# A four-layer image network on one core: ScalarE's allowance for side work made to depend on the kinds of neighbouring scan units

## The chip, the core and the metric

The kernel runs on one core of a Trainium2 chip. The metric is device time in microseconds (us), the median of several executions. The engines are called as in the profile: PE (TensorE), DVE (VectorE), ACT (ScalarE), POOL (GpSimd) and SP (the queue that issues the transfers).

## The reference

The input is `x`, four images of 96 channels and 64 x 64 pixels, in f32. Four layers follow each other, each adding to its input. Layer 0 dominates. It is a selective scan over the 4096 pixels of an image, in four directions `k` (by rows, by columns, and both reversed), with 192 channels and 16 states for each channel:

```python
u = silu(depthwise_conv3x3(Win @ groupnorm(x)))           # 192 channels
dts, Bs, Cs = split(sel_w[k] @ u_in_direction_k)          # 6 + 16 + 16
delta = softplus(dt_w[k] @ dts + dt_b[k])
for l in range(4096):                                     # per direction
    h = h * exp(delta[l] * A) + (delta[l] * u[l]) * B[l]  # 192 x 16 states
    y[k][l] = sum_over_states(h * C[l]) + Ds[k] * u[l]
x = x + Wout @ layernorm(y[0] + y[1] + y[2] + y[3])
```

Layer 1 is an inverted bottleneck (96 to 576 channels, depthwise 3x3, back to 96). Layer 2 is a Fourier filter along the pixels and a feed-forward block in 8-bit floats. Layer 3 is a linear attention and another such block.

## The kernel before

**The scan.** The recurrence runs on DVE's scan instruction. The time axis of 4096 pixels is cut into 8 chunks of 512. A *step* is one chunk of one direction of one image, so there are 4 x 4 x 8 = 128 steps. A step has 12 *units*; a unit covers 32 channel pairs and 4 states, as two tiles of 128 x 512 (`e` = 0 and 1). There are 1536 units, and one *slot* for each. The order of instructions in a slot is written out by hand and is the same on every engine's queue:

- `decays` of the next unit: two ACT exponentials (L1284) into two PSUM banks `ps_da`, of which there are four. Before each, ACT copies the last state of the unit before, if that unit is of the long kind (L1308).
- `sums_out` (L1346 on): if a sum over states is finished, ACT copies it from the bank `ps_y` to `yt` (L1352), and two stores to HBM are queued.
- `inputs` of the unit after the next: one POOL product `db` (L1274).
- `product` of the unit two slots back, if it is a unit of POOL's: POOL multiplies by C (L1314).
- `states` of this unit: two DVE scans (L1293), and, if the unit isn't POOL's, two DVE products by C (L1298).
- `sums`: four PE matmuls per unit sum over the states (L1338).

So there are two kinds of units. A *long* one has two scans and two products on DVE. A *short* one (POOL's, `POOL_C`: units 1, 3, 5, 7 and 10 of each 12) has two scans alone. Kinds alternate almost strictly: of 12 slots, five are long before short, five short before long and two long before long.

**The side work.** Everything else, that is the front of layer 0 (convolution, projections), its output, and layers 1 to 3, is written as Python generators called *streams*, in *stages* that run one after another: `front`, `turn` (brings the column directions back to rows), `conv` (layer 0's output, then layer 1), `spectral`, `layer_2`, `layer_3`; `layer_3_turn` runs a turn beside a layer 3. Each stream yields, for its next piece, the engine and an estimated cost. At the end of a slot `advance` places pieces of the first stage as long as they fit:

```python
            for e, (us, most) in SHARE.items():
                room[e] = min(room[e] + us, most)
...
            owed = min(owed + rate, 8.0)
            while owed > 0.0:
                did = advance(stages)
```

Each engine has a `room`, which grows in each slot by a first number of `SHARE` and is capped by the second. A piece needs a room of at least half its cost, and takes its whole cost off it. A stream may use one engine only in a slot, save that an ACT piece may follow its own PE piece. `rate` is the cost of the work that remains, divided by the slots that remain, and at least 6.0. The side work of the last image that depends on its last direction (`behind`, the last `conv`) starts when all before it is placed.

**The tail.** What is not placed when the 1536 units are through is issued after them by `force`, with no limits but the banks; all eight PSUM banks are then open to it. It holds what is left of the last `conv`, and the last image's `spectral`, `layer_2` and `layer_3`.

Of the kernel before, what the change touches and what calls it, by code (L numbers as in the profile page):

```python
# [53 lines left out]
WORK = {"weights": 47.0, "turn": 70.0, "front": 417.0, "conv": 447.0,  # L54
        "spectral": 111.2, "layer_2": 231.0, "product": 1.2, "layer_3": 153.6, "layer_3_turn": 223.6}
RATE = 6.0
SHARE = {"pe": (3.0, 3.2), "act": (2.4, 2.8), "dve": (1.5, 2.0)}
NQ, NG, NPAIR = 4, HID // 32, H // 2


# [35 lines left out]
def hybrid_kernel(ctx: ExitStack, tc: tile.TileContext, a: dict):  # L96


    pe, ac, dv = ((lambda us, banks=0, ind=False, e=e: (e, us, banks, ind)) for e in ("pe", "act", "dve"))
# [3 lines left out]
    act = nc.scalar.activation  # L103
# [3 lines left out]
    pool = lambda name, bufs=1, **kw: ctx.enter_context(tc.tile_pool(name=name, bufs=bufs, **kw))  # L107
# [329 lines left out]
    def later(out, t, then=None):  # L437

        to_store.append((out, t, then))

    def flush():
        while to_store:
            out, t, then = to_store.pop(0)
            store(out, t)
            if then is not None:
                then()
# [769 lines left out]
    def scans(stages):  # L1216
# [12 lines left out]
        units = []  # L1229
# [23 lines left out]
        def need(step):  # L1253

            while (step["k"] % 2, step["c"]) not in traced[step["b"]]:
                force(stages)
            flush()
# [5 lines left out]
        def fetch(step, what):  # L1263
            for name, i in what:
                if name == "BC":
                    load_states(step, i)
                else:
                    load_channels(step, i, name)
# [3 lines left out]
        def inputs(x):  # L1272
            x["db"] = pair("db")
            nc.gpsimd.tensor_mul(x["db"], x["step"]["g"][x["i"]], both(x["step"]["BC"][x["j"]][:, 0]))  # L1274

        def decays(x, last):
            x["da"] = []
            for e in (0, 1):

                if last is not None and not last["pool"]:  # L1280
                    keep(last, e)
                av = (x["step"]["k"] * NI + 2 * x["i"] + e) * NJ + x["j"]
                x["da"].append(bank("da"))
                act(x["da"][e], x["step"]["d"][x["i"]][:, e], AF.Exp, scale=aneg[:, av : av + 1])  # L1284

        def states(x):
            step, u = x["step"], x["u"]
            order = slice(None, None, -1) if step["k"] >= 2 else slice(None)
            x["hc"] = pair("hc")
            x["h"] = [x["hc"][:, e] for e in (0, 1)] if x["pool"] else x["da"]  # L1290
            for e in (0, 1):
                start = 0.0 if step["n"] == 0 else steps[x["number"] - 1]["last"][:, 2 * u + e : 2 * u + e + 1]
                nc.vector.tensor_tensor_scan(  # L1293
                    x["h"][e][:, order], x["da"][e][:, order], x["db"][:, e, order], start, ALU.mult, ALU.add
                )
            if not x["pool"]:
                for e in (0, 1):
                    x["made"] = nc.vector.tensor_mul(x["hc"][:, e], x["h"][e], x["step"]["BC"][x["j"]][:, 1])  # L1298
# [13 lines left out]
        def product(x):  # L1312
            keep(x, 0)
            x["made"] = nc.gpsimd.tensor_mul(x["hc"], x["hc"], both(x["step"]["BC"][x["j"]][:, 1]))  # L1314
# [3 lines left out]
        def through(b):  # L1318
            scanned[b] += 1
# [7 lines left out]
        def sums(group):  # L1327
            step, first, last = group[0]["step"], group[0]["j"] == 0, group[1]["j"] == NJ - 1
            if first:
                step["y"] = bank("y")  # L1330
            y = step["y"]

            made = None
            for m in (1, 0):
                x = group[m]
                for e in (1, 0):
                    q = 2 * m + e
                    done = mm(y[32 * q : 32 * q + 32], lhsT=const("stack"), rhs=x["hc"][:, e],  # L1338
                              start=first or (x["pass"] == 0 and x["j"] == 0), stop=last or (x["pass"] == 0 and x["j"] == NJ - 1))
                    if made is None:  # L1340
                        made = group[0]["made"]
                        tc.add_manual_dep(done.ins, made.ins.name, mybir.DependencyInfo(
                            mybir.DependencyClass.Sync, mybir.DependencyReason.DATA), reason="sums")
            if last:
                summed.append((group, y))

        def sums_out():
            while summed:
                group, y = summed.pop(0)
                step = group[0]["step"]  # L1350
                yt = sp.tile([128, CH], F32, name="yt")
                nc.scalar.copy(yt, y)  # L1352
                to = d_y[step["k"]][step["b"] % 2][step["c"]]
                for m in (0, 1):
                    at = 128 * group[0]["pass"] + 64 * m
                    later(to[at : at + 64].rearrange("(p e) l -> e p l", e=2), yt[64 * m : 64 * m + 64],
                          (lambda b=step["b"]: through(b)) if group[0]["pass"] == 1 and m == 1 else None)
# [11 lines left out]
        for slot in range(len(units) + 6):  # L1369
            clock[0] = slot  # L1370
            x = units[slot] if slot < len(units) else None
            if x is not None:
                if x["u"] == 0:


                    last = len(units) - NCH * PC
                    if slot < last:
                        rate = max(RATE, sum(s.work for s in stages if s not in behind) / (last - slot))
                    else:
                        rate = sum(s.work for s in stages) / (len(units) - slot)  # L1380
                if x["number"] > 0 and PC + x["u"] in LOADS:
                    fetch(x["step"], LOADS[PC + x["u"]])
                if x["number"] + 1 < len(steps) and x["u"] in LOADS:
                    if x["u"] == 4:
                        need(steps[x["number"] + 1])
                    fetch(steps[x["number"] + 1], LOADS[x["u"]])
            flush()
            if slot + 1 < len(units):
                decays(units[slot + 1], units[slot - 1] if slot > 0 else None)
            sums_out()  # L1390
            if slot + 2 < len(units):
                inputs(units[slot + 2])
            if 2 <= slot < len(units) + 2 and units[slot - 2]["pool"]:
                product(units[slot - 2])
            if x is not None:
                states(x)
            for group in due.get(slot, ()):
                sums(group)
            for e, (us, most) in SHARE.items():
                room[e] = min(room[e] + us, most)  # L1400
            tensor[0] = 0.0
            held_banks[0] -= freed[0]
            freed[0] = 0
# [3 lines that stand above are left out]
                if did is None:  # L1407
                    break
                owed -= did
# [1 line left out]


    clock, tensor = [-1], [0.0]
    room = {e: most for e, (_, most) in SHARE.items()}

    class Stage:

# [41 lines left out]
    def advance(stages):  # L1459

        while stages and not stages[0].fill():
            stages.pop(0)
        if stages:
            banks_left = BANKS["mm"] - held_banks[0]
            for stream in stages[0].active:
                engine, us, banks, _ = stream["next"]
                if banks and banks > banks_left:

                    banks_left = 0
                elif fits(stream):  # L1470
                    if engine != "wait":
                        room[engine] -= us
                    if engine == "pe":
                        tensor[0] += us
                    return stages[0].step(stream)
        return None
# [18 lines left out]
    with tc.manual_schedule(engines={nc.tensor.engine, nc.scalar.engine, nc.vector.engine, nc.gpsimd.engine, nc.sync.engine}):  # L1495
        scans(stages)
# [154 lines left out]
```

## Time and profile before

| what | us |
|---|---|
| median of 3 runs | 6392.89 (6386.30 to 6405.43) |
| the profiled execution, its own time | 6409.81 |
| its span in the profile | 6408.0 |
| first scan starts, last scan ends, from the span's start | 78.6, 5976.2 |
| two scans of a unit | 2 x 1.27 |
| two products by C on DVE, of a long unit | 2 x 0.67 |
| two exponentials on ACT | 2 x 0.69 |
| `db` on POOL, one of each unit | 2.37 |
| copy of `y` on ACT | 0.58 |

The profile is one execution. A group's line gives the source line, the engine, the tiles written and read, the number of instructions, then the busy time and the mean of one, and at last the engine's idle time just before these instructions and who ended it. A line of the waits gives who waited, for whom, the total, the number of times and the longest. A matmul of f32 appears as two records in the trace. A window's line gives the busy time and the number of records of each engine, the granted clock of PE, the share of the DMA engines and their rate. SP issues all transfers of the kernel.

### The profile page before, as it was taken

The numbers are of one execution on the slowest core, as the hardware profiler recorded it, in microseconds if no ns is written. First come the engines' busy times: TensorE is split into PE (matmuls) and PEld (weight loads), VectorE is DVE, ScalarE is ACT, GpSimd is POOL, SyncE is SP. The second block draws the span as 40 slices with busy tenths as digits, with TensorE's granted clock in tenths as the row PEclk, the third lists the DMA queues.
The fourth block names the chain that finished last, engine by engine and source line by source line (L and its number), as shares of the span: only waits on it lengthen the run. The fifth ranks groups of instructions, "written<-read, shape, count | busy, mean of one in ns | idle before, by whom it ended". The sixth has DMA issues, their size and how long they took to land. (4 is left out here: it accounts for less than half of the span.)

```text
span 6408.0 us, 84715 instructions
## 1 busy us (share of the span) xinstructions
PE 4763.2 (74%) x27804; PEld 1766.1 (28%) x27804; DVE 5488.4 (86%) x6059; ACT 4178.6 (65%) x8040; POOL 5171.1 (81%) x2743
## 2 busy tenths in 40 slices
PE   6633767757987776686589877767988786867998
PEld 2100212111223532121122254211223632112274
DVE  5979898988999889999899988988999889799345
ACT  5743777765675677887566667856675677665435
POOL 4757878878999889987999988987999888899200
PEclk9855978868998877797799988878998877878999
DMA  5644565666644544456775455465644545555201
GB/s 186 210 159 148 184 205 194 200 222 230 190 158 157 193 161 144 162 195 213 250 222 170 150 180 174 144 213 186 195 161 153 198 157 174 185 188 181 95 11 42
DMA packets 434365, 1112.01 MB, mean 174 GB/s; under 512 B 72474, under 2 KB 74240, under 8 KB 432772
## 3 DMA queue, kind: packets, MB, share of 16 engines
q1 hardware_dynamic: 433924, 1106.58, 52.5%
q8 instruction: 221, 3.62, 0.2%
q14 instruction: 220, 1.80, 0.1%
HBM read 873.41 MB, written 237.44 MB: 173 GB/s over the span
## 5 line engine op out<-in xcount | busy, mean ns | idle before, releaser
L1274 POOL TENSOR_TENSOR db<-rep_g,rep_BC 128x1024 f32<-128x1024 f32 x1536 | 3608.6, 2365 | 753.4 <-DVE hc L1293 352.1
L1284 ACT ACTIVATE ps_da<-rep_d,aneg 128x512 f32<-128x512 f32 x3072 | 2062.6, 690 | 460.1 <-DVE hc L1293 351.1
L1293 DVE TENSOR_TENSOR_SCAN ps_da<-ps_da,state,db 128x512 f32<-128x512 f32 x1568 | 1922.4, 1271 | 284.8 <-ACT state L1308 166.3
L1314 POOL TENSOR_TENSOR hc<-hc,rep_BC 128x1024 f32<-128x1024 f32 x640 | 1511.0, 2361 | 48.5 <-DVE hc L1293 3.7
L1293 DVE TENSOR_TENSOR_SCAN hc<-ps_da,state,db 128x512 f32<-128x512 f32 x1120 | 1370.8, 1264 | 135.2 <-issue 41.7
L1338 PE MATMUL ps_y<-hc,cst 128*32 128x512 f32 x6144 | 1004.1, 732 | 524.2 <-POOL hc L1314 215.6
L1298 DVE TENSOR_TENSOR hc<-ps_da,rep_BC 128x512 f32<-128x512 f32 x1792 | 1133.7, 673 | 0.2
L1308 ACT COPY state<-ps_da 128x1 f32<-128x1 f32 x1568 | 247.3, 158 | 452.9 <-DVE hc L1298 452.1
L1338 PEld LDWEIGHTS ps_y<-hc,cst 128*32 128x32 f32 x6144 | 147.3, 118 | 1173.2 <-issue 484.6
L818 PE MATMUL ps_mm<-h,wd 128*32 128x512 f32 x3144 | 359.9, 593 | 7.0 <-ACT r L155 7.0
L552 PE MATMUL ps_mm<-xp,taps 128*128 128x512 f32 x576 | 292.2, 651 | 47.6 <-ACT xp L532 14.2
L1293 DVE TENSOR_TENSOR_SCAN ps_da<-ps_da,db 128x512 f32<-128x512 f32 x224 | 261.0, 1210 | 28.4 <-ACT state L1308 14.3
L795 PE MATMUL ps_mm<-wd,w 128*32 128x512 f32 x2016 | 255.4, 622 | 27.6 <-DMA wd<-x 17.0
L603 PE MATMUL ps_mm<-xd,dtw 128*128 128x512 f32 x256 | 167.4, 745 | 71.1 <-ACT z L625 51.8
L1293 DVE TENSOR_TENSOR_SCAN hc<-ps_da,db 128x512 f32<-128x512 f32 x160 | 186.1, 1203 | 22.9 <-issue 16.4
L877 PE MATMUL ps_mm<-r,cst 128*128 128x512 f32 x214 | 148.9, 785 | 55.8 <-ACT acc L900 20.3
L799 ACT ACTIVATE h<-ps_mm 128x512 f32<-128x512 f32 x267 | 155.7, 596 | 51.9 <-PE ps_mm L795 49.3
L705 PE MATMUL ps_mm<-ypart,cst 128*128 128x512 f32 (+1 forms) x272 | 158.0, 704 | 38.1 <-DMA ypart<-yt 37.4
L990 PE MATMUL ps_mm<-wa,xp 128*64 128x96 f32 x1728 | 135.1, 318 | 66.2 <-DVE d L995 56.6
L618 DVE SCALAR_TENSOR_TENSOR ps_mm<-ps_mm,z 128x512 f32<-128x512 f32 x192 | 131.3, 684 | 60.5 <-ACT z L616 57.7
L612 ACT ACTIVATE z<-ps_mm 128x512 f32<-128x512 f32 x192 | 114.2, 595 | 96.6 <-PE ps_mm L603 48.2
L552 PEld LDWEIGHTS ps_mm<-xp,taps 128*128 128x128 f32 x576 | 115.4, 207 | 222.0 <-issue 158.8
(343 smaller groups left out, 6824.3 us busy)
## 6 DMA issues: line engine op xcount, KB each, us to landing
rep_BC<-bc SPq DMA_DIRECT2D x512, 512.0 KB
rep_g<-du SPq DMA_DIRECT2D x384, 512.0 KB
rep_d<-delta SPq DMA_DIRECT2D x384, 512.0 KB
y<-yt SPq DMA_DIRECT2D x512, 128.0 KB
du<-g SPq DMA_DIRECT2D x128, 256.0 KB
delta<-z SPq DMA_DIRECT2D x128, 256.0 KB
tab<-in_etab SPq DMA_DIRECT2D x112, 256.0 KB
ypart<-y SPq DMA_DIRECT2D x72, 256.0 KB
```

The costliest lines, as they stand in the source:

```text
L552: mm(p, lhsT=taps[:, t, 0:128], rhs=window(t, c + e), start=t == 0, stop=t == 8)
L603: mm(p, lhsT=dtw[:, o + 2 * part, 0:128], rhs=xd, start=True, stop=True)
L705: mm(p, lhsT=const(name, slice(0, s.shape[0])), rhs=s, start=n == 0, stop=n == len(of) - 1)
L795: mm(p[32 * n : 32 * n + 32], lhsT=w1[:, 32 * g : 32 * g + 32], rhs=xin[:, n : n + 15 : 2, 1 : W + 1], start=True, stop=True)
L818: mm(p[32 * n : 32 * n + 32], lhsT=held["wd"][:, groups[i], o, dx, :], rhs=here[i][:, :, dx : dx + W], start=dx == 0, stop=dx == 2)
L1274: nc.gpsimd.tensor_mul(x["db"], x["step"]["g"][x["i"]], both(x["step"]["BC"][x["j"]][:, 0]))
L1284: act(x["da"][e], x["step"]["d"][x["i"]][:, e], AF.Exp, scale=aneg[:, av : av + 1])
L1293: nc.vector.tensor_tensor_scan(x["h"][e][:, order], x["da"][e][:, order], x["db"][:, e, order], start, ALU.mult, ALU.add)
L1298: x["made"] = nc.vector.tensor_mul(x["hc"][:, e], x["h"][e], x["step"]["BC"][x["j"]][:, 1])
L1308: nc.scalar.copy(to[:, e : e + 1], x["h"][e][:, end : end + 1])
L1314: x["made"] = nc.gpsimd.tensor_mul(x["hc"], x["hc"], both(x["step"]["BC"][x["j"]][:, 1]))
L1338: done = mm(y[32 * q : 32 * q + 32], lhsT=const("stack"), rhs=x["hc"][:, e], start=first or (x["pass"] == 0 and x["j"] == 0), stop=last or ...
```

## The change

ACT's entry leaves `SHARE` for a table by the kind of this unit and of the next (True is a POOL unit, that is a short one). A short unit before a long one gives 2.8 and a cap of 3.0; a long before a short 1.2 and 1.6; the others stay at 2.4 and 2.8. The copy of `y` now takes 0.6 from ACT's room. Nothing else is edited.

```diff
-SHARE = {"pe": (3.0, 3.2), "act": (2.4, 2.8), "dve": (1.5, 2.0)}
+SHARE = {"pe": (3.0, 3.2), "dve": (1.5, 2.0)}
+SHARE_ACT = {(True, False): (2.8, 3.0), (True, True): (2.4, 2.8), (False, False): (2.4, 2.8), (False, True): (1.2, 1.6)}
...
                 nc.scalar.copy(yt, y)
+                room["act"] -= 0.6
...
-            for e, (us, most) in SHARE.items():
+            of = (x is not None and x["pool"], slot + 1 < len(units) and units[slot + 1]["pool"])
+            for e, (us, most) in (SHARE | {"act": SHARE_ACT[of]}).items():
                 room[e] = min(room[e] + us, most)
...
-    room = {e: most for e, (_, most) in SHARE.items()}
+    room = {e: most for e, (_, most) in SHARE.items()} | {"act": 2.8}
```

Lines of the kernel after stand one lower than before from L58 on, and two lower behind the copy of `y`.

## The prediction

> **What bounds the kernel now.** I read the page's busy times first, then a table of windows around the end of the scans, then the waits of VectorE. The page:
>
> ```profile
> PE 4763.2 (74%) x27804; PEld 1766.1 (28%) x27804; DVE 5488.4 (86%) x6059; ACT 4178.6 (65%) x8040; POOL 5171.1 (81%) x2743
> ```
>
> DVE is fullest, but the average hides two regimes. The windows (busy of PE, PEld, DVE, ACT, POOL; PE's clock; DMA share; GB/s) show them:
>
> ```profile
> 5700.00:5800.00 100.00, 55.77 (x180) 15.43 (x181) 95.19 (x100) 53.94 (x113) 98.97 (x54) 0.70 0.59 190
> 5900.00:5976.00 76.00, 67.35 (x360) 20.18 (x363) 68.40 (x74) 47.42 (x87) 63.67 (x32) 0.96 0.43 135
> 5976.00:6105.00 129.00, 124.21 (x798) 37.25 (x794) 10.47 (x19) 46.23 (x73) 0.00 (x0) 0.99 0.26 83
> 6105.00:6230.00 125.00, 121.80 (x1922) 100.65 (x1916) 54.53 (x72) 35.60 (x50) 0.00 (x0) 0.99 0.04 11
> 6230.00:6408.00 178.00, 152.43 (x1301) 91.06 (x1296) 100.74 (x214) 93.47 (x154) 0.00 (x0) 0.96 0.13 38
> ```
>
> Up to 5976 us the scans run, and DVE and POOL set the pace: side work on PE or ACT lies beside them. Behind 5976 is the tail, 432 us, and PE is busy for 398 of them. **A microsecond of PE work is nearly free in the first regime and costs a microsecond in the second.** This carries the forecast.
>
> In the scans DVE is busy 5307 of 5898 us and idle 591. The waits (total, times, longest) name ACT for 325 of these:
>
> ```profile
> DVE ps_da L1293 <- ACT state L1308: 180.7, 102, 9.5
> DVE ps_da L1293 <- ACT ps_da L1284: 92.0, 48, 7.5
> ...
> DVE hc L1293 <- ACT ps_da L1284: 34.6, 18, 3.6
> ...
> DVE hc L1293 <- ACT state L1308: 17.5, 7, 4.5
> ```
>
> ACT is late with its exponentials because a piece of side work stands before them in its queue. Often that piece is short but itself waits for PE:
>
> ```profile
> ACT yrow L669 <- PE ps_mm L665: 153.4, 46, 14.6
> ACT yrow L708 <- PE ps_mm L705: 100.9, 46, 7.1
> ACT r L874 <- PE ps_mm L871: 100.8, 55, 14.3
> ```
>
> **What the Trainium skill says.** "PSUM — Partial Sum Buffer", Engine vs sequencer instructions: the queues of ScalarE, VectorE and GpSimd are strictly first in, first out, and matmuls start and complete in program order. The trace agrees: a copy L669 of 0.58 us that waited 14.6 us for PE (unit 308) made DVE wait 9.5 us. "Perfetto Trace Analysis", Optimization Strategy: a kernel can have several regimes with different busiest engines; here DVE at 90%, then PE at 92%. "TensorE: Matmul & The Clock Gate", Part 3, The mechanism: matmuls in different column groups run concurrently; here 24 records of L818, each about 0.6 us long, pass in 2.76 us, so I price such lines by span and not by duration.
>
> **The change, part by part.** (1) *How much ACT work may be placed.* Per 12 slots the allowance goes from 12 x 2.4 = 28.8 to 5 x 2.8 + 5 x 1.2 + 2 x 2.4 = 24.8; two copies of y take 1.2, so 23.6, less 18%. Nothing waits for the allowance as such, but pieces that don't fit slip to a later slot. (2) *Where it is placed.* I went through both built orders slot by slot and priced ACT's side pieces (and the copy of y) by the durations of their lines in the trace. Long before short: 930 us before, 622 after. Short before long: 785, then 948. Long before long: 309, then 346. The sum falls from 2024 to 1916: **108 us of ACT work no longer finds a slot.** (3) *Where that goes.* In the built order of the kernel after, the last `layer_3_turn` begins at slot 1510, before at 1392; the last `conv` began at slot 1450 and now has no slot at all. `rate` rises (to about 15 at slot 1488), but the missing room is ACT's, so it can't catch up. All that slipped goes to the tail, where PE pays.
>
> *The tail.* Behind the last exponential of the scans PE has 2102 instructions before and 2622 after. The extra, priced by what a line's instruction (two records in f32) takes of PE in the trace:
> - second half of `turn`: L662 16 x 2.07 (its strided reads make it double), L664 and L665 16 x 0.95: 48 us
> - `scan_outputs`: L705 35 x 1.05; L724 to L742 56 x 0.95: 90 us
> - `conv`: L795 136 x 0.25, L818 180 x 0.22 (12 in 2.6 us), L834 and L835 10 x 0.9: 83 us
> - norms L871, L877 11 x 0.95, the previous image's feed-forward, 8-bit L897 and L918 27 x 0.35 (the other half of their counts is weight loads), and 5 others: 24 us
>
> Sum **245 us**. It also brings idle PE that had been hidden under the scans. The second half of `turn` reads 2 x 2 MB before its first matmul, at 190 to 315 GB/s (the windows' rates) 13 to 22 us; then stores and reloads through HBM between `turn`, `scan_outputs` and `conv`; the first `conv` block needs three chunks of `scan_outputs`, each a chain of PE and ACT in turns with no other PE work to fill in, where one reload cost PE 3.7 us in the tail before. From below nothing more than 20 us, from above 70; I take 45. SP only issues these transfers earlier or later; nothing in the tail queues behind the scans' loads, since they are over. ACT and DVE have 175 and 166 us of work in 432: the extra there (141 and 61 instructions of about 0.6 us) lies beside PE. **Tail: +290 us.**
>
> *The scans.* About 30 DVE side instructions of 0.65 us leave (61 more in the tail, but 31 of these stand for ACT's): -20 us, since DVE is the bound. For ACT's lateness I took, for each slot of the trace, its kind, its ACT side work in bins of 0.7 us, and DVE's wait for ACT before the unit that follows:
>
> | slot | slots | wait us | wait per slot by bin of 0.7 us |
> |---|---|---|---|
> | long, short | 640 | 207 | 0.10 0.21 0.28 0.62 0.52 2.36 |
> | short, long | 639 | 96 | 0.08 0.07 0.18 0.26 1.07 1.11 |
> | long, long | 256 | 19 | 0.03 0.01 0.07 0.24 0 0 |
>
> So the change does take work from the worse place. With the bins of the order after (long-short 245, 278, 106, 11, 0, 0; short-long 217, 124, 89, 127, 74, 8) the same rates give 119 + 163 + 18 = 300 us against 317: -16. But 74 slots now have 2.8 to 3.5 us in the short-long place, a bin with a handful of samples before; at the rate of the bin beneath it they cost 20 us instead of 79, and the gain is -76. I take -45, keep both ends, and add -10 for waits on PE that go with the side work. A straight line through the 128 steps (step time against side work) gives about 0.75 us for each us of DVE and 0.1 for ACT, so 15 + 11 = 26 us. **Scans: -75 us** (-25 to -170).
>
> Sum: +290 - 75 = +215. The profiled execution took 6409.8 us (span 6408.0), which is 17 above the median; so 6393 + 215 = **6608 us**.
>
> **The rivals.**
> - *All of ACT's lateness goes.* The most that placement can give is 323 us; with 20 for DVE and 10 for PE the scans lose 353, the net is -63: 6330 us, **faster**. It decides if the scans shorten by over 290 us. For it: 207 of the wait is in the long-short slots, which is just where work is cut. Against: 125 of those 207 stand behind side work that itself waited over 1 us for another engine, mostly PE, which ACT's allowance doesn't touch, and the work reappears in the slot next to it.
> - *The long-short waits go and nothing else worsens:* -207 - 30 + 290 = +53: 6446 us.
> - *The allowance doesn't bind*, and it is all a reshuffle: about 6393 us. ACT's side work averages 1.3 us a slot against 2.4, which speaks for it; the built order, with 520 more PE instructions in the tail, against.
> - *A worse tail:* if the chain of `turn`, `scan_outputs` and `conv` leaves PE idle for 120 us instead of 45, 6680 us.
>
> **How the numbers follow.** The likeliest case 0.78, its own range 6500 to 6690. All lateness gone 0.05; long-short alone 0.07; reshuffle 0.03; worse tail 0.07. The range 6480 to 6700 leaves out most of the second to fourth. About 0.3% (19 us) is what a measurement of this kernel can tell from no change: faster 0.06, same 0.04, slower 0.90.
>
> **What would show it.** Right: the last scan ends near 5900, the tail is 700 to 740 us with PE busy over 85% of it, L662 and all of L795's last 288 matmuls stand behind the last scan, and DVE's wait for ACT is 240 to 310. Wrong: a last scan before 5690, or a tail under 600 us, or PE idle for over 120 us in it.

## The result and the profile after

The kernel after takes **6447.31 us** (median of 5 runs, 6440.44 to 6451.89) against 6396.65 us before (5 runs). The ratio is 1.0075, with a 95% interval of 1.0064 to 1.0087: slower by 0.75%, some 50 us. The forecast had the direction right and the size wrong: +215 us, with a range that began at 6480. In the experiments below, one execution of uniform (13504 us) and one of thin_dense (10949 us) stand far apart from the others of their kernel, for a reason that no trace shows; the ratios leave them out.

The page's busy times after, and the windows of the kernel after around the end of its scans (busy of PE, PEld, DVE, ACT, POOL, then PE's clock, DMA share, GB/s):

```profile
PE 4757.2 (74%) x27786; PEld 1747.5 (27%) x27786; DVE 5487.7 (85%) x6090; ACT 4159.0 (65%) x8009; POOL 5167.7 (80%) x2743
```
```profile
78.00:5777.00 5699.00, 4092.61 (x22766) 1430.02 (x22766) 5277.62 (x5697) 3872.02 (x7553) 5156.00 (x2735) 0.82 0.57 186
5777.00:6438.00 661.00, 616.57 (x4897) 297.57 (x4894) 195.55 (x365) 259.46 (x415) 0.53 (x1) 0.99 0.21 62
```
```profile
5777.00:5900.00 123.00, 108.08 (x245) 36.88 (x246) 23.83 (x52) 41.49 (x72) 0.53 (x1) 0.98 0.68 200
5900.00:6150.00 250.00, 250.00 (x1575) 74.29 (x1568) 16.44 (x28) 95.42 (x149) 0.00 (x0) 1.00 0.12 34
```

Weight loads apart, no engine's total differs by as much as 0.5% from before, so the totals say nothing here. The place says all. The last scan ends at 5777.4 us, 199 us earlier than before. The tail behind it takes 661.3 us, 229 more than the 431.8 of before, and PE is busy for 616 of them: in 250 us on end (the last window shown) it never rests. Both effects are large and of opposite sign; what is measured is their difference. The profiled executions, spans of 6408.0 and 6438.7 us, show +31 of the medians' +51.

DVE's waits for ACT in the scans, after (the answers to the four lines of before):

```profile
DVE ps_da L1294 <- ACT state L1309: 65.9, 44, 6.0
DVE ps_da L1294 <- ACT ps_da L1285: 62.0, 33, 6.8
...
DVE hc L1294 <- ACT ps_da L1285: 29.3, 20, 4.4
...
DVE hc L1294 <- ACT state L1309: 10.5, 3, 4.3
```

They add up to 168 us, where they were 325. Of the three lines of ACT's own waits for PE that the prediction showed, one grew (153.4 us before; 157 of the 174.0 fall in the scans, the rest in the tail):

```profile
ACT yrow L670 <- PE ps_mm L666: 174.0, 47, 13.6
...
ACT r L875 <- PE ps_mm L872: 87.9, 57, 13.6
...
ACT yrow L709 <- PE ps_mm L706: 62.6, 35, 4.4
```

### The profile page after: what moved, and what is told of

Its sections match the earlier page's. It is cut to its first block, busy times and chain, and to the rows that moved or that the text cites. A ratio compares the mean times of both kernels' runs of the same rounds, so it can differ in the third digit from the quotient of the medians.

```text
span 6438.7 us, 84655 instructions
## 1 busy us (share of the span) xinstructions
PE 4757.2 (74%) x27786; PEld 1747.5 (27%) x27786; DVE 5487.7 (85%) x6090; ACT 4159.0 (65%) x8009; POOL 5167.7 (80%) x2743
## 5 line engine op out<-in xcount | busy, mean ns | idle before, releaser
L1339 PE MATMUL ps_y<-hc,cst 128*32 128x512 f32 x6144 | 1024.7, 747 | 651.6 <-ACT yt L1353 263.6
L819 PE MATMUL ps_mm<-h,wd 128*32 128x512 f32 x2904 | 336.1, 596 | 7.6 <-ACT r L156 7.6
L796 PE MATMUL ps_mm<-wd,w 128*32 128x512 f32 x1728 | 217.6, 613 | 20.1 <-ACT h L800 11.3
L1034 PE MATMUL ps_mm<-z,tab 128*128 128x96 f32 x864 | 136.6, 326 | 52.3 <-DMA tab<-in_etab 37.9
```

What stands on the lines that cost most here:

```text
L796: mm(p[32 * n : 32 * n + 32], lhsT=w1[:, 32 * g : 32 * g + 32], rhs=xin[:, n : n + 15 : 2, 1 : W + 1], start=True, stop=True)
L819: mm(p[32 * n : 32 * n + 32], lhsT=held["wd"][:, groups[i], o, dx, :], rhs=here[i][:, :, dx : dx + W], start=dx == 0, stop=dx == 2)
```

## The experiments

Each was timed beside the kernel before on the same chip. The diffs of the first part are against the kernel after, those of the others against y_only unless the text says otherwise; so all but kinds_only and act23 have the debit of 0.6 for the copy of y. "Tail's PE work by the planner's costs" is what the built program still has to place on PE behind the scans. The measured numbers of all, in us (last scan, tail and wait are of the profiled executions; DVE's wait for ACT is that before a unit's first scan, without the very first unit, and so up to 4 us less than a sum of the views' lines):

| kernel | median | ratio to before (95%) | last scan ends | tail | wait for ACT | tail's PE work |
|---|---|---|---|---|---|---|
| before | 6393 to 6398 | | 5976 | 432 | 323 | 378 |
| after | 6447 | 1.0075 (1.0064 to 1.0087) | 5777 | 661 | 165 | 592 |
| y_only | 6348 | 0.9926 (0.9905 to 0.9947) | 5916 | 441 | 281 | 384 |
| kinds_only | 6474 | 1.0120 (1.0100 to 1.0140) | 5839 | 632 | 228 | 553 |
| uniform | 6430 | 1.0052 (1.0033 to 1.0070) | 5820 | 610 | 258 | 546 |
| reversed | 6436 | 1.0063 (1.0045 to 1.0081) | 5768 | 670 | 196 | 599 |
| pe24 | 6462 | 1.0110 (1.0081 to 1.0139) | 5785 | 666 | 178 | 593 |
| pe_more | 6516 | 1.0191 (1.0166 to 1.0216) | 5966 | 553 | 344 | 502 |
| y_pe36 | 6486 | 1.0142 (1.0114 to 1.0169) | 6063 | 428 | 392 | 366 |
| u22_pe36 | 6444 | 1.0076 (1.0052 to 1.0100) | 6011 | 430 | 375 | 366 |
| act28 | 6366 | 0.9960 (0.9951 to 0.9969) | 5929 | 432 | 293 | 378 |
| act23 | 6381 | 0.9979 (0.9972 to 0.9987) | 5941 | 439 | 294 | 384 |
| pe28_act28 | 6355 | 0.9940 (0.9921 to 0.9960) | 5917 | 432 | 257 | 383 |
| pe26_act32 | 6373 | 0.9967 (0.9952 to 0.9982) | 5913 | 454 | 260 | 400 |
| hold_conv | 6518 | 1.0189 (1.0174 to 1.0205) | 5905 | 612 | 268 | 544 |
| thin_dense | 6307 | 0.9857 (0.9837 to 0.9877) | 5868 | 437 | 212 | 366 |

### First: the parts of the change, and its place

**y_only** is the debit without the kinds.

```diff
-SHARE_ACT = {(True, False): (2.8, 3.0), (True, True): (2.4, 2.8), (False, False): (2.4, 2.8), (False, True): (1.2, 1.6)}
+SHARE_ACT = {(True, False): (2.4, 2.8), (True, True): (2.4, 2.8), (False, False): (2.4, 2.8), (False, True): (2.4, 2.8)}
```

> The debit of 0.6 for the copy of y alone; every slot keeps 2.4 with a cap of 2.8. In the built order the tail's PE work is nearly that of before (384 us by the planner's own costs against 378; after: 592), so the tail should be about 438 us. If the debit is what took the 58 us of waits out of the slots with a copy of y (79 before, 21 after), the last scan ends near 5920 and the kernel takes about 6345 us. If those waits went because of the smaller allowance in the long-before-short slots, where both copies stand, the last scan stays within 20 us of 5976 and the time within 20 us of before.

6348 us, faster than before by 0.74%; the last scan ends at 5916. The tail is nearly that of before (441 us). So the loss of the change lies in the table by kinds, which takes the kernel from 6348 to 6447. But the waits in slots that hold a copy of y fell from 79 to 67 only, so these slots are not where most of it was gained.

**kinds_only** is the table without the debit.

```diff
                 nc.scalar.copy(yt, y)
-                room["act"] -= 0.6
```

> The table by kinds alone, without the debit for the copy of y. Tail's PE work 553 by the planner's costs, so a tail near 620 us. If the kinds make the gain, the last scan ends near 5800 and the kernel takes about 6440 us, as the kernel after. If the debit makes 50 us or more of it, the last scan ends near 5840 and the time is about 6475 us.

6474 us, near the second figure: the debit is worth 27 us on top of the kinds, and 50 alone.

**uniform** gives every slot the average of the table.

```diff
-SHARE_ACT = {(True, False): (2.8, 3.0), (True, True): (2.4, 2.8), (False, False): (2.4, 2.8), (False, True): (1.2, 1.6)}
+SHARE_ACT = {(True, False): (2.07, 2.4), (True, True): (2.4, 2.8), (False, False): (2.07, 2.4), (False, True): (2.07, 2.4)}
```

> The allowance of the kernel after on average, but the same in every slot (2.07, cap 2.4), with the debit. ACT's side work stands half in long-before-short slots (793 by the planner's costs, 811 in short-before-long), as before; sums of two neighbouring slots over 4.5 us are 73 instead of 239 (after: 97). Tail's PE work 546, so a tail near 612 us. If the place within the pair matters, the waits for ACT stay at 250 us or more, the last scan ends near 5890 and the time is about 6520 us. If the sum over neighbouring slots is what matters, the waits fall to about 165 us, the last scan ends near 5785 and the time is about 6410 us.

Neither in full. The waits for ACT are 258 us, as the theory of the place had it, but the last scan ends at 5820 us, nearer to the other. At 6430 us it is a little faster than the kernel after. Its scans are 96 us shorter than those of y_only, and the column of waits accounts for only 23 of these. DVE also waits for ACT before its own pieces of side work, 61 us in y_only and 17 here, and has 16 us less work.

**reversed** gives more where the next unit is short, and less where it is long.

```diff
-SHARE_ACT = {(True, False): (2.8, 3.0), (True, True): (2.4, 2.8), (False, False): (2.4, 2.8), (False, True): (1.2, 1.6)}
+SHARE_ACT = {(True, False): (1.2, 1.6), (True, True): (2.4, 2.8), (False, False): (2.4, 2.8), (False, True): (2.8, 3.0)}
```

> The table the wrong way round: 1.2 (cap 1.6) in a short unit's slot before a long one, 2.8 (cap 3.0) in a long unit's slot before a short one, with the debit. ACT's side work is 985 in the long-before-short slots by the planner's costs and 561 in the others; sums of two neighbouring slots over 4.5 us are 75. Tail's PE work 599, a tail near 668 us. If the place matters, DVE's waits for ACT are 320 us or more, the last scan ends at 5950 or later and the time is over 6630 us. If the sum matters, the waits are near 165 us, the last scan ends near 5780 and the time is about 6455 us.

6436 us, and the last scan ends at 5768: the table the wrong way round does what the table the right way round does (6447 and 5777). **Where in a pair of slots ACT's work stands does not set the time.** What the two have in common is the amount that ACT may take. The windows of reversed, to be laid beside those of after:

```profile
78.00:5767.00 5689.00, 4089.16 (x22755) 1438.12 (x22754) 5285.91 (x5697) 3865.10 (x7545) 5157.78 (x2735) 0.82 0.56 186
5767.00:6437.00 670.00, 625.70 (x4903) 300.88 (x4903) 197.32 (x367) 263.35 (x423) 0.81 (x1) 0.98 0.20 61
```

### Second: ACT's bursts, or PE

**pe24** leaves ACT its old allowance and cuts PE's.

```diff
-SHARE = {"pe": (3.0, 3.2), "dve": (1.5, 2.0)}
+SHARE = {"pe": (2.4, 2.6), "dve": (1.5, 2.0)}
```

> ACT's allowance as before (2.4, cap 2.8, in every slot) with the debit for the copy of y, but PE's cut from 3.0 to 2.4 (cap 2.6), so that as much side work slips to the tail as in the kernel after (593 us of PE by the planner's costs; after 592, debit alone 384). Sums of ACT's side work over two neighbouring slots above 4.5 us stay frequent (178; debit alone 209, after 97). If the shorter scans come from the mere amount of side work that left, the last scan ends near 5777 and the time is about 6440 us. If they come from ACT's bursts being cut, the last scan ends near 5880 and the time is about 6540 us.

The last scan ends at 5785 and the waits for ACT are 178 us, with ACT free to burst nearly as before (ACT's planned work of two neighbouring slots exceeds 4.5 us 178 times, against 97 in the kernel after). The idea that cutting ACT's bursts is what shortened the scans falls: as much came of a limit on PE. Under this limit ACT's wait for PE in the turn was 96 us, where it was 153 before, but that alone can't be the cause either, since the kernel after has scans as short with 174. What both kernels share is the amount of side work that left the scans; the fourth part takes this apart. pe24's line:

```profile
ACT yrow L670 <- PE ps_mm L666: 95.8, 32, 10.5
```

**pe_more** raises PE's allowance in the kernel after, **y_pe36** does the same in y_only, and **u22_pe36** cuts ACT's bursts besides, by the second pair of lines.

```diff
-SHARE = {"pe": (3.0, 3.2), "dve": (1.5, 2.0)}
+SHARE = {"pe": (3.6, 3.8), "dve": (1.5, 2.0)}
...
-SHARE_ACT = {(True, False): (2.4, 2.8), (True, True): (2.4, 2.8), (False, False): (2.4, 2.8), (False, True): (2.4, 2.8)}
+SHARE_ACT = {(True, False): (2.2, 2.4), (True, True): (2.4, 2.8), (False, False): (2.2, 2.4), (False, True): (2.2, 2.4)}
```

> The kernel after with PE's allowance raised from 3.0 to 3.6 (cap 3.8); ACT's table by kinds stays. Tail's PE work falls from 592 to 502 by the planner's costs, so a tail near 565 us (after: 661). Neighbouring sums above 4.5 us: 120 (after 97). If bursts set the waits, the last scan ends near 5800 and the time is about 6370 us. If the amount sets them, each us that comes back out of the tail costs about 0.65 us of scans: last scan near 5840, 6410 us. If more PE work in a slot makes ACT wait for PE, it is 6440 us or more.

> The debit alone, with PE's allowance 3.6 (cap 3.8). Tail's PE work 366 by the planner's costs, a tail near 425 us; neighbouring sums above 4.5 us 218, as with the debit alone. Control for the next kernel: PE's allowance by itself should leave the last scan within 25 us of 5916; about 6340 us. If the fuller slots of PE hold up ACT, the last scan ends near 5960 and the time is 6390 us.

> The debit, ACT's allowance 2.2 with a cap of 2.4 in every slot, PE's 3.6 (cap 3.8). Tail's PE work 366 by the planner's costs, no more than before, and neighbouring sums above 4.5 us 96, as few as in the kernel after. If ACT's bursts over neighbouring slots set the waits, DVE's wait for ACT falls to about 200 us, the last scan ends near 5840, the tail is 425 us and the time about 6265 us, faster than both. If the amount of side work sets them, the last scan stays near 5916 and the time is about 6340 us.

6516, 6486 and 6444 us. The first and second went the way of their last branch, PE holding up ACT, and further than I gave it; the third met neither of its figures. PE's allowance of 3.6 alone made the scans 147 us longer than in y_only and the waits for ACT 392 us, and fewer bursts of ACT took only 17 of these waits away again. Its scans are 51 us shorter than those of y_pe36 all the same, with the same tail, so ACT's allowance does count where PE's is this wide. ACT's wait in the turn is the largest of all kernels in these three; y_pe36 first, then pe_more:

```profile
ACT yrow L670 <- PE ps_mm L666: 236.8, 58, 13.1
```
```profile
ACT yrow L670 <- PE ps_mm L666: 253.7, 63, 13.6
```

### Third: amounts and allowances near those of before

The edits, in this order: **act28** (ACT up), **act23** (ACT's allowance down by as much as the debit takes, and no debit), **pe28_act28** and **pe26_act32** (PE down, ACT up). Only the lines as they read after the edit are shown.

```diff
+SHARE_ACT = {(True, False): (2.8, 3.2), (True, True): (2.4, 2.8), (False, False): (2.8, 3.2), (False, True): (2.8, 3.2)}
```
```diff
-                room["act"] -= 0.6
+SHARE_ACT = {(True, False): (2.3, 2.7), (True, True): (2.4, 2.8), (False, False): (2.3, 2.7), (False, True): (2.3, 2.7)}
```
```diff
+SHARE = {"pe": (2.8, 3.0), "dve": (1.5, 2.0)}
+SHARE_ACT = {(True, False): (2.8, 3.2), (True, True): (2.4, 2.8), (False, False): (2.8, 3.2), (False, True): (2.8, 3.2)}
```
```diff
+SHARE = {"pe": (2.6, 2.8), "dve": (1.5, 2.0)}
+SHARE_ACT = {(True, False): (3.2, 3.6), (True, True): (2.4, 2.8), (False, False): (3.2, 3.6), (False, True): (3.2, 3.6)}
```

> The debit, with ACT's allowance raised to 2.8 (cap 3.2) in every slot, PE's at 3.0. By the planner's costs ACT's sums over two neighbouring slots exceed 4.5 us 310 times (debit alone 209), PE's exceed 6 us 252 times (248), and the tail's PE work is 378 (384). If PE's crowding in a slot sets ACT's lateness, nothing much moves: last scan within 30 us of 5916, about 6350 us. If ACT's own bursts set it, DVE waits for ACT 350 us or more, the last scan ends near 5990 and the time is about 6420 us.

> No debit for the copy of y and no kinds: ACT's allowance is 2.3 (cap 2.7) in every slot, which takes as much off per 12 slots as the debit does (1.2). Tail's PE work 384 by the planner's costs, the same as with the debit alone. If the debit gained by the amount that it takes off, about 6350 us, within 25. If it gained by sparing the slots with a copy of y, within 20 us of before.

> The debit, PE's allowance down to 2.8 (cap 3.0), ACT's up to 2.8 (cap 3.2) in every slot. Tail's PE work 383 by the planner's costs, as with the debit alone; PE's sums over two neighbouring slots exceed 6 us 102 times (debit alone 248), ACT's exceed 4.5 us 297 times (209). If PE's crowding sets ACT's lateness, DVE's waits for ACT fall to about 220 us, the last scan ends near 5860, the tail is 440 and the time is about 6300 us. If ACT's bursts set it, the last scan ends beyond 5960 and the time is 6400 us or more. If only the amount of side work counts, it is the debit alone again, about 6350 us.

> The same further on: PE's allowance 2.6 (cap 2.8), ACT's 3.2 (cap 3.6), with the debit. Tail's PE work 400 by the planner's costs; PE's sums over two slots exceed 6 us 54 times, ACT's exceed 4.5 us 305 times. If PE's crowding sets ACT's lateness, the last scan ends near 5830, the tail is about 457 and the time about 6287 us. If ACT's bursts set it, 6420 us or more. If only the amount counts, about 6350 us.

act28 (6366 us) has half as many bursts of ACT again as y_only and is only 19 us slower. pe28_act28 (6355) is y_only again, in time and in last scan, although sums of PE over two slots exceed 6 us 102 times instead of 248. pe26_act32 (6373) is no faster, although its wait in the turn is small:

```profile
ACT yrow L670 <- PE ps_mm L666: 62.2, 21, 11.6
```

So with PE's allowance between 2.6 and 3.0, ACT's between 2.4 and 3.2 and the debit kept, the number of bursts of either engine, counted over all slots alike, moves the time by 25 us at most; at 3.6 for PE that no longer holds, as seen above. act23 takes off as much as the debit, with the same tail, and is at 6381: 14 us below before, and so within the 20 that were to speak for the slots with a copy of y. But the waits in those slots had fallen by 12 us only. **What the debit gains is not settled:** by amount alone 14 us, with the debit 50. act28, pe28_act28 and pe26_act32 lie 7 to 25 us from y_only, so the debit's gain is not far above what a small difference of the built order does here.

### Fourth: less side work in the scans, or the same spread thinner

By then the last scan seemed to follow the amount that had left for the tail: from y_only (384, 5916) over uniform (546, 5820) to after (592, 5777), about 0.6 to 0.7 us for each us of the tail's PE work. Two readings were open: a slot without side work is shorter, or the stages that are most dense, being held back, are spread over more slots.

**hold_conv** takes work out without spreading any: the last `conv` waits until the scans are over.

```diff
-            while owed > 0.0:
+            while owed > 0.0 and not (stages and stages[0] in behind):
```

> The debit alone, but the last conv is not begun before the scans are through: the last 64 slots carry no side work and all earlier slots carry what they carry with the debit alone. Tail's PE work 544 by the planner's costs, as with the same allowance in every slot (546, last scan 5820 us). If the scans shorten by the mere amount of side work that leaves them (0.7 us for each us of the tail's PE work), the last scan ends near 5805, the tail is about 612 and the time about 6420 us. If they shorten because the dense stages (front, spectral, layer_2, layer_3) are spread over more slots, these are as dense as ever here: the last scan ends at 5890 or later and the time is about 6500 us.

6518 us, last scan 5905: the same 160 us of PE work in the tail, and the scans lose only 10 us. **The mere amount of side work that leaves does not shorten the scans:** `conv`, which left here, is nearly free in them. The 63 slots at the end that carry no side work at all take 3.32 us each, and those with `conv` 3.36. The windows of hold_conv (the border is 4 us behind its last scan):

```profile
78.00:5909.00 5831.00, 4173.18 (x22919) 1432.62 (x22922) 5303.25 (x5711) 3922.59 (x7635) 5157.81 (x2735) 0.81 0.56 183
5909.00:6517.00 608.00, 559.70 (x4764) 278.23 (x4756) 176.47 (x319) 230.83 (x364) 0.00 (x0) 0.96 0.17 49
```

**thin_dense** spreads without taking out: PE's allowance by stage.

```diff
-            for e, (us, most) in (SHARE | {"act": SHARE_ACT[of]}).items():
+            for e, (us, most) in (SHARE | {"act": SHARE_ACT[of], "pe": (3.6, 3.8) if stages and stages[0].name == "conv" else (2.7, 2.9)}).items():
```

> The debit alone, with PE's allowance 2.7 (cap 2.9) in all stages but conv, and 3.6 (cap 3.8) in conv. Tail's PE work 366 by the planner's costs, no more than before. If spreading the dense stages is what shortens the scans, front, spectral, layer_2 and layer_3_turn take fewer us per slot than the 4.10, 3.90, 3.66 and 4.11 of the debit alone, DVE's wait for ACT falls to about 230 us, the last scan ends near 5865 and the time is about 6295 us. If the amount in the scans alone counts, it is the debit alone again (5916, 6345 us). If conv at 3.6 crowds PE as 3.6 everywhere did (6486 us), conv takes over 3.5 us per slot instead of 3.37 and the time is 6400 us or more.

6307 us: faster than before by 1.4%, and than the kernel after by 2.2% (6307 / 6447). It is the fastest kernel of this study. The tail is nearly that of before, and the last scan ends 108 us earlier, at 5868 where the first branch had 5865. Its waits, DVE for ACT and ACT in the turn:

```profile
DVE ps_da L1294 <- ACT state L1309: 138.8, 87, 6.8
...
DVE ps_da L1294 <- ACT ps_da L1285: 55.2, 36, 4.0
```
```profile
ACT yrow L670 <- PE ps_mm L666: 31.3, 19, 3.9
```

To see where, I gave each slot the stage that it served, by the built order, and took its length from scan to scan in the trace (the row of `conv` in hold_conv includes its last slots without side work):

| stage | before: slots, us each | after | hold_conv | thin_dense |
|---|---|---|---|---|
| front | 351, 4.18 | 408, 3.93 | 366, 4.09 | 372, 4.04 |
| turn | 93, 3.74 | 92, 3.90 | 92, 3.76 | 108, 3.33 |
| conv | 486, 3.40 | 405, 3.37 | 465, 3.35 | 436, 3.53 |
| spectral | 196, 3.96 | 222, 3.72 | 197, 3.91 | 198, 3.85 |
| layer_2 | 192, 3.75 | 214, 3.46 | 197, 3.68 | 201, 3.58 |
| layer_3_turn | 122, 4.20 | 94, 4.01 | 123, 4.07 | 125, 3.79 |

A slot without side work takes 3.32 us (hold_conv). What a stage adds to this is its slots times the difference, and from before to after it changed by: front -53 us, layer_2 -53, spectral -37, layer_3_turn -42, `conv` -19, turn +14. The sum, -190, is nearly the 199 by which the scans became shorter. Front, spectral and layer_2 do the same work in more slots, and these are shorter; they make up 143 us. The turn, which ACT's allowance does not hold back, saves nothing. Part of `conv` and of layer_3_turn left for the tail; how much of the 42 comes from what left, and how much from thinner slots, no run separates, since hold_conv moved `conv` alone.

In thin_dense the changes against before are: layer_3_turn -49 us, turn -38, front -34, layer_2 -30, spectral -20, and the denser `conv` +53, in sum -118 where the scans lost 108. Of front, spectral and layer_2, y_only has a part too (4.10, 3.90 and 3.66 us for each slot). Here no work left for the tail that stood in the scans before, so thinning out the dense stages does shorten the scans by itself.

Why the turn gains can be read from the built orders. A piece of the turn is four matmuls, two of L662 and two shorter ones, 5.15 us of PE in the tail of the kernel after (the lines stand in the last section), which its stream announces as 3.8. It needs a room of 1.9. With 3.0 and a cap of 3.2 the room behind such a piece is 3.2 - 3.8 + 3.0 = 2.4, and the next slot takes another. With 2.7 and 2.9 it is 1.8, and the next slot must pass. So in y_only 32 of the 64 pieces stand in the slot right behind another, in y_pe36 51, in thin_dense, pe26_act32 and pe24 none, and ACT's wait in the turn goes with it: 137 and 237 us, then 31, 62 and 96. That pe26_act32 is not faster for it fits its ACT allowance of 3.2: spectral took fewer slots there, and longer ones (178 of 4.11 us, 198 of 3.85 in thin_dense). No run separates the two halves of thin_dense, 2.7 for the other stages and 3.6 for `conv`.

## Why the prediction was wrong in size, point by point

- **The direction, and the mechanism in the tail: right.** The table lets less ACT work into the scans, side work slips by over a hundred slots, and the last `conv` ends up behind the scans, where PE pays. hold_conv shows that price by itself: 160 us of PE work moved, 171 us more tail, 10 us shorter scans. But the sign hung on a smaller margin than forecast: two terms of 229 and 199 us, where 290 and 75 were expected.
- **The tail's PE work: 245 us forecast, 218 measured** (398 to 616 us busy). All terms were a little high: turn 48 against 41, outputs 90 against 77, conv 83 against 77, the rest 24 against 20. For the turn the reason can be seen: 2.07 us is the sum of a matmul's two records in the trace, which overlap, and from one start to the next an L662 took 1.71 us, and the shorter ones 0.87 instead of 0.95.
- **Idle PE in the tail: 45 us forecast, 12 measured** (33.6 to 45.1), below the lower end of 20. The chain of `turn`, `scan_outputs` and `conv` was to leave PE waiting. In the trace it is covered: in the first 123 us of the tail PE is busy for 108, since what was left of the previous image's layer 3 fills in. Together the tail was 290 in the forecast and 229 in the result.
- **The scans: -75 us forecast, -199 measured. This is the step that failed.** The DVE work that left was 30 us (forecast 20). DVE's waits for ACT fell by 158 us, where the prediction took 45, and 76 at the most; its waits for ACT before side pieces fell by 22 more, and its other waits grew by some 10. The 199 lies outside the prediction's own range for the scans, which ended at 170. Too little gain here (124 us) and too much loss in the tail (61) make up the whole distance from +215 to the +31 of the profiled executions. The method was at fault: it took the wait of a slot as a function of that slot's own kind and ACT work, and carried the rates of before over to the order after. The rates did not carry over: for a short-long slot with 2.8 to 3.5 us of work, 1.07 us of wait before (7 slots only) and 0.21 after (85 slots); for a long-short one with 0.7 to 1.4 us, 0.21 before and 0.08 after. The reading that fits is that a wait builds up over the slots before it, and these had become thinner; no run isolates it. The straight line through the 128 steps, carried over in the same way, gave 26 us. (The sum of 300 us should have been set against the 322 of its own table, not 317: -22 instead of -16, which changes little.)
- **"A PE wait that ACT's allowance doesn't touch": wrong for most stages.** The waits behind side work that itself waited over 1 us went from 235 to 151 us. A stream alternates PE and ACT, so a limit on ACT thins out its PE work too. For the turn alone the sentence holds: 153 us before, 174 after, 157 of them in the scans.
- **That taking work "from the worse place" makes the gain: no.** The waits did stand mostly behind long-short slots (207 of 323 us), but reversed, with more of ACT's pieces there than before (1080 us by their durations, against 930), has scans as short as the kernel after. That waits show behind a kind of slot did not mean that work had to leave that kind.
- **The rival "the long-short waits go and nothing else worsens"** was put at 6446 us, within 2 us of the result. Its amount was right by chance: the waits fell by 133 us in the long-short slots and by 24 elsewhere, and the tail was cheaper than it assumed.
- **The signs it set itself.** PE's share in the tail (93%) and the work that would stand there (L662, L795's 288 matmuls) came as it said. The last scan (5777, not near 5900), the tail (661, not 700 to 740) and the wait for ACT (168, not 240 to 310) did not, and yet none of its signs of being wrong appeared: they were set too far out to show a miss of this size.

## What to carry to other kernels

Where side work is dealt out to the slots of a main loop, the sum over the loop and what is left behind it must be counted together: an allowance that shortens the loop by 199 us is worth nothing if it sends 218 us of PE work to a place with no cover. Ask then which stages are dense, and hold back those, with room given to the stage that costs the loop little; the two limits here that held in every stage and shortened the loop by some 190 us, ACT's table and pe24, pushed over 200 us of PE work out of it. Look at announced costs too: a piece that takes more than it announces can stand in every slot where it should stand in every second. And don't carry a table of "wait per slot" from one order to another: here the same bin of work had 0.21 us of wait for each slot in one order and 0.08 in the other.

## What the runs showed of the hardware

One piece of the turn in the tail of the kernel after, where PE's granted clock was 0.99 (from 5775 to 5800 us), and the start of the next piece:

```profile
5786.19 1.88 PE L663 MATMUL ps_mm<-ya,cst 128*128 128x512 f32 x2
5787.89 1.90 PE L663 MATMUL ps_mm<-yb,cst 128*128 128x512 f32 x2
5789.60 1.04 PE L665 MATMUL ps_mm<-ya,cst 128*128 128x512 f32 x2
5790.48 1.02 PE L666 MATMUL ps_mm<-yb,skips 128*128 128x512 f32 x2
5791.34 1.88 PE L663 MATMUL ps_mm<-ya,cst 128*128 128x512 f32 x2
```

A matmul of 128 x 512 in f32 whose moving operand is read with a stride of 64 elements (L662 before, L663 after, pixels by column) took 1.70 and 1.71 us from its start to the next one's, against 0.88 and 0.86 for those read straight on: about double. There are 128 such instructions in the kernel, and the copy behind them has ACT's largest waits for PE.

PE's granted clock was 0.99 on average over the 661 us of tail with PE busy for 93% of it, while in the scans it was 0.82 at 72% busy.
